# A hand-ordered four-layer kernel: the end of an LSTM reordered, and one event list across a batch norm

## The chip, the cores and the metric

One core of one Trainium2 chip. The metric is the device time of one launch in microseconds; lower is better. Engines in the text: PE (TensorE, the matrix array), DVE (VectorE), ACT (ScalarE), POOL (GpSimd), SP (SyncE, which issues most DMAs).

## What is computed

A residual tower of four layers over x, 128 batches of 64 nodes with 256 features, in float32. Each layer is `x = x + GNN(relu(layernorm(x)))`. The change lies at the end of layer 0 and in layer 1:

```python
# layer 0, its last part: LSTMs over windows of p nodes, p = 1..4
for p in range(1, MAX_SKIP + 1):
    nw = Tv // p
    wins = h[:, :nw * p, :].reshape(Bv * nw, p, Hd)
    last = _lstm_last(Wih[p - 1], Whh[p - 1], bih[p - 1], bhh[p - 1], wins)
    h = h.at[:, jnp.arange(nw) * p + (p - 1), :].set(last.reshape(Bv, nw, Hd))
#   one step:  i, f, g, o = split(x_t @ Wih.T + h @ Whh.T + bias)
#   c = sigmoid(f) * c + sigmoid(i) * tanh(g);   h = sigmoid(o) * tanh(c)

# layer 1, A_hat = the adjacency, normalized by degrees
agg = einsum("nm,bmd->bnd", A_hat, features)
h = relu(batchnorm(agg @ W1.T + b1))      # 256 -> 512, statistics over all 8192 rows
out = batchnorm(h @ W2.T + b2)            # 512 -> 256
```

Layers 2 and 3 (a graph convolution and causal attention) follow and are not touched. A batch norm needs the statistics of all rows before any row can go on: nothing of W2 can start on a channel until that channel is complete.

## The kernel before

**Tiles.** The 8192 rows are 16 super-tiles of 512 rows. Activations of layers 0 and 1 lie with channels on the partitions, in chunks of 128; each chunk of a super-tile is a 128x512 tile. The 256-wide hidden state has two chunks, the 512-wide middle of layer 1 four (numbered 0 to 3), handled in two halves (g = 0: chunks 0 and 1; g = 1: chunks 2 and 3). Matrix products of two super-tiles with a 256x256 block of weights are done in a scheme of seven products where eight would be plain. It needs sums of the weights (weight_sum, line 301 ff.: four POOL operations per weight) and of the data (T1 to T4: ag_sums at line 801 ff., and `sums` in second_product). The products carry numbers 1 to 7 and gather in three PSUM banks called a, b and c; DVE and ACT move the banks out in between (evict, add).

**Order.** There is no automatic scheduler. Events are put in a list by `at(t, fn)` with a time chosen by hand, sorted, and issued in that order; each engine then works through its own queue in order, and waits for data or for a free buffer. A time in the list decides only the order within each queue.

**LSTM.** `step` (line 717 ff.) does one time step for one state, a pair of blocks of 512 columns: the gates i, g, f, o one after another (`gate`: products on PE at L665 and L671, adds on DVE at L687, sigmoid and tanh on ACT at L683), then the cell: for each half n of the state, a multiply `keep` and an add `plus` (both at L710), tanh of the cell (L715), and `state` (L635), which writes h into the array hT that layer 1 reads. The operations of L710 run on POOL. Where `turn` is set (the last step of p = 2 and p = 3), DVE takes half n = 1. For p = 4 `turn` is always False. The last step of p = 4 on the second pair of groups ends the LSTM.

**The beginning of layer 1** is in the same list, behind `t -= 28` (line 792): `begin(s, t_load, t_turn, t_stats, t_relu, t_agg)` handles the first super-tiles of the class First: load x, transpose on PE (L541), add to x on DVE (L547), store, statistics on DVE (L564, L565), `root` (two operations on DVE at L569 and L570, two on POOL at L571 and L572), relu on ACT, aggregate on PE (L585). Super-tile 3 is turned at 30.6 and its statistics are taken at 36.1, between ag_sums of pair 0 (35.3, four sums on DVE, L810) and the last h (L635).

**Layer 1.** Products with W1 are in `half(i, g)` for pair i = 0 to 7: products L905, evictions by ACT L910, adds L913 and statistics L916 on DVE, in a rhythm GATE of 8.7 us per half; the last of the seven products of each half lies in the next half's time. PSUM is split in a pool of 5 banks ("gates") for these and one of 3 ("rest") for transposes and aggregates. After the last pair, `bn_coeffs` (L857 to L863) computes scale and shift for two chunks at a time: two bn_aggr, an add, three further small operations on DVE, and a power of -0.5 on POOL (L860). Then that list is issued, PSUM is made into one pool of 8 banks, weights of the later layers are loaded, and a second list holds the products with W2: `second_product(i)` has relu on ACT (L991; four operations on DVE at L987 and L989 in pair 0), the sums T1, T2, T3, T4 (L999 to L1005, for k = 0 on DVE, for k = 1 on POOL, except pair 0, all on DVE), products L1015 (k = 0 and k = 1: first and second half of the 512 channels), evictions L1019, adds L1022, statistics L1028. bn_coeffs of the second batch norm and layer 2 follow (L1078, L1112, L1121, L1173). The weight sums of W2 (L303) are issued on POOL just ahead of layer 1's list.

Of the kernel before, what the change touches and what calls it, by code (L numbers as in the profile page):

```python
# [14 lines left out]
P = 128  # L15
# [5 lines left out]
def kernel(ctx: ExitStack, tc: tile.TileContext, a: dict, out: bass.AP):  # L21
# [83 lines left out]
    mhalf = const.tile([P, 8], F32, tag="mhalf", name="mhalf")  # L105
    nc.gpsimd.memset(mhalf, -0.5)

    def block_diag(name, src):
# [490 lines left out]
    def at(t, fn, *args):  # L599
        events.append((t, len(events), fn, args))  # L600
# [116 lines left out]
    def step(t0, st, j, last, l, w, short_next):  # L717
# [20 lines left out]
        else:  # L738
# [4 lines left out]
            e, when, h_at = end["f"], (0, 6 * u, 11 * u), t + 8.6  # L743
            if short_next:
                keep_ = both(nc.vector.tensor_mul, st, "c", g["f"], "c")
                plus_ = both(nc.vector.tensor_add, st, "c", "c", g["g"])
                when, h_at = (0.4, 11.0, 12.0), t + 14.3
            for n in range(2):
                at(end["g"] + 0.1 * n, mul, n)
                at(e + when[0] * n, (keep, keep_)[n], n)  # L750
                at(e + when[0] * n + 0.1, (plus, plus_)[n], n)
# [20 lines left out]
    for p in range(1, NL + 1):  # L772
        l = p - 1
        if p < NL:
            at(t + 7.5, load, l + 1, 0)
            at(t + (40 if p == 1 else 64), lambda l=l: weight_sums(wt[l + 1][0][0]))
        if p > 1:
            at(t + 7.5, load, l, 1)
        whh_due = p > 1
        pairs = pairs_of(p)  # L780
        for k in range(0, len(pairs), 2):
            sts = [{"blk": blk, "N": blk[0][2] * GB, "p": p, "pool": pool}
                   for blk, pool in zip(pairs[k : k + 2], (lh0, lh1))]
            for j in range(p):
                for st in sts:
                    if j and whh_due:
                        whh_due = False
                        at(t - 6, lambda l=l: weight_sums(wt[l][1][0]))
                    turn = j == p - 1 and 1 < p < NL and k + 2 >= len(pairs)
                    t = step(t, st, j, j == p - 1, l, wt[l], turn)  # L790
# [21 lines left out]
    def begin(s, t_load, t_turn=None, t_stats=None, t_relu=None, t_agg=None):  # L812
# [8 lines left out]
        def stats():  # L821
            for q in range(Q):
                f.stats(q)
            f.root()

# [16 lines left out]
    begin(2, 13, 22.9, 23.0, 27.2)  # L842
    begin(3, 17, 30.6, 36.1)
    begin(4, 23)
    for k in range(4):
        at(t + 35.3 + 0.1 * k, ag_sums, 0, k, nc.vector)
# [5 lines left out]
    def bn_coeffs(pool, co, stats, c0, c1, prm, name):  # L852
# [10 lines left out]
        nc.vector.tensor_sub(shift, prm[:, 2, c0:c1], shift)  # L863

    co1 = const.tile([P, 3, HC], F32, tag="co1", name="co1")
    co2 = const.tile([P, 3, KC], F32, tag="co2", name="co2")
# [4 lines left out]
    with tc.tile_pool(name="pz", bufs=1, reuse_waits="tile") as pz:  # L871
# [8 lines left out]
        st2 = pz.tile([P, KC, NS, 6], F32, tag="st2", name="st2")  # L880
        for k in range(4):
            weight_sum(w2, k)

        new_banks(gates=5, rest=3)
        GATE = 8.7
        events = []

# [3 lines left out]
        def half(i, g):  # L893
# [23 lines left out]

            for t, name, j in ((0, "c", 2), (1.72, "a", 1), (3.46, "b", 5), (4.32, "a", 6),
                               (6.07, "b", 3), (6.93, "a", 7), (GATE + 0.86, "a", 4)):
                at(t0 + t, product, name, j)  # L920
            for t, fn, n, o, name in ((2.75, evict, 0, 0, "a"), (3.5, add, 0, 0, "c"),
                                      (4.5, evict, 1, 1, "b"), (5.35, evict, 1, 0, "a"),
                                      (7.1, add, 1, 0, "b"), (7.95, add, 1, 1, "a"),
                                      (GATE + 1.9, evict, 0, 1, "a")):
                at(t0 + t, fn, n, o, name)
            for t, n, o in ((5.5, 0, 0), (9.0, 1, 0), (9.7, 1, 1), (GATE + 2.9, 0, 1)):
                at(t0 + t, stats, n, o)
            if i == NS // 2 - 1:
                at(t0 + GATE + 3, bn_coeffs, lns, co1, st1, 2 * g, 2 * g + 2, con["bn1"], "bn1")

        for i in range(NS // 2):
            for g in range(2):
                half(i, g)
            for k, t in enumerate((-4.3, 0.9, 2.2, 3.5) if i else ()):
                at(GATE * 2 * i + t, ag_sums, i, k, nc.vector if i == NS // 2 - 1 else nc.gpsimd)
        for s in range(2, NS):
            f, t0 = First(s, "rest"), GATE * s
# [19 lines left out]

        for _, _, fn, args in sorted(events, key=lambda e: e[:2]):
            fn(*args)
        new_banks(psum=8)  # L960
        front.close()
        last.close()
        late = ctx.enter_context(tc.tile_pool(name="late", bufs=1, side="right", reuse_waits="tile"))
        adj4 = load_const("adj4", parts_d, [P, 4, P], late)
        adj3, smask = adj4[:, 0:3, :], adj4[:, 3, :]
        wl2 = [weight(f"wl2_{k}", a["W"][k], late) for k in range(3)]
        bl2 = row_bcast("bl2", a["bias"], D, late)
        wqk = late.tile([P, KC, D], F32, tag="wqk", name="wqk")
        aqk = late.tile([P, 7, P], F32, tag="aqk", name="aqk")
        wvo = late.tile([P, KC, D], F32, tag="wvo", name="wvo")  # L970
        wqkv = weight("wqkv", a["Wqkv"], late)
        wo = weight("wo", a["Wo"], late)

        events = []

        def second_product(i, tp):


            t0 = 7.0 * i
            tt, banks = {}, {}  # L980
# [3 lines left out]

            def relu(n, c):
                if i == 0 and n == 1 and c % 2 == 0:
                    nc.vector.tensor_scalar(z(n, c), z(n, c), co1[:, 0, c : c + 1],  # L987
                                            co1[:, 1, c : c + 1], op0=ALU.mult, op1=ALU.add)
                    nc.vector.tensor_scalar_max(z(n, c), z(n, c), 0.0)  # L989
                else:  # L990
                    nc.scalar.activation(z(n, c), z(n, c), AF.Relu, bias=co1[:, 1, c : c + 1],  # L991
                                         scale=co1[:, 0, c : c + 1])

            def sums(name, k, engine):
                if name != "T3" and name not in tt:
                    tt[name] = tp.tile([P, 2, SUP], F32, tag=name, name=name)
                b11, b21, b12, b22 = (z(n, 2 * k + c) for n in range(2) for c in range(2))
                if name == "T1":
                    engine.tensor_sub(tt["T1"][:, k], b12, b11)  # L999
                elif name == "T2":  # L1000
                    engine.tensor_sub(tt["T2"][:, k], b22, tt["T1"][:, k])
                elif name == "T3":
                    engine.tensor_sub(b12, b22, b12)
                else:
                    engine.tensor_sub(tt["T4"][:, k], b21, tt["T2"][:, k])  # L1005

            def product(name, j, ks=(0, 1)):
                new = name not in banks
                if new:
                    banks[name] = bank()  # L1010
                for k in ks:
                    x_ = (z(0, 2 * k), z(0, 2 * k + 1), z(1, 2 * k + 1),
                          *(tt[v][:, k] if v in tt else None for v in ("T4", "T1", "T2")),
                          z(1, 2 * k))[j - 1]
# [15 lines left out]
            def at(t, fn, *args):  # L1030
                events.append((t0 + t, len(events), fn, args))

            for k, (n, c) in enumerate(((0, 1), (0, 0), (0, 3), (0, 2), (1, 0), (1, 2), (1, 1), (1, 3))):
                at((-6.3, -5.8, -5.3, -4.4, -3.9, -3.4, -2.4, -1.9)[k], relu, n, c)
            for k, engine in enumerate((nc.vector, nc.gpsimd if i else nc.vector)):
                for name, t in (("T1", -2.8), ("T2", 0.1), ("T3", 0.6), ("T4", 1.6)):
                    at(t, sums, name, k, engine)
            for t, name, j in ((0, "c", 2), (1, "a", 1), (3, "b", 5), (5, "a", 6), (9, "a", 7),
                               (11, "b", 3), (13, "a", 4)):
                if i == 0 and t < 2:  # L1040
                    at(t, product, name, j, (0,))
                    at(t + 1.1, product, name, j, (1,))
                else:
                    at(t, product, name, j)
            at(2.2, lambda: evict(y(0, 0), 0, "a"))
            at(3.1, lambda: add(y(0, 0), y(0, 0), "c"))
            at(3.6, stats, 0, 0)
            at(4, lambda: evict(y(1, 1), 1, "b"))
            at(6, lambda: evict(tt["T2"][:, 0], 0, "a"))
            at(10, lambda: add(y(1, 1), y(1, 1), "a"))  # L1050
            at(10.5, stats, 1, 1)
            at(12, lambda: add(y(1, 0), tt["T2"][:, 0], "b"))
            at(12.5, stats, 1, 0)
            at(14.2, lambda: evict(y(0, 1), 1, "a"))
            at(15, stats, 0, 1)

        with tc.tile_pool(name="tp", bufs=2, reuse_waits="tile") as tp:
            for i in range(NS // 2):
                second_product(i, tp)
            for _, _, fn, args in sorted(events, key=lambda e: e[:2]):  # L1060
                fn(*args)
        bn_coeffs(lns, co2, st2, 0, KC, con["bn2"], "bn2")

# [355 lines left out]
```

## Time and profile before

| | |
|---|---|
| median of 3 runs | 1885.29 us (1885.29 to 1886.8) |
| profiled execution | 1886.4 us |
| its span, first to last instruction | 1884.5 us |
| mean granted TensorE clock | 0.997 |
| PE waits named in the trace, L905 (first batch norm's products) | 2.5 us and 1.9 us |
| PE waits on L1015 (products with W2) | 1.5 us and 0.9 us |
| bn_aggr (L857), 128x96 | 0.55 us each |
| pow on POOL (L860), 128x2 | 0.70 us |
| cell operation (L710) on POOL, 128x1024 | 2.35 us median |

In the trace all times are in microseconds from the start of the span. The LSTM's last products end at about 1218, layer 1's products with W1 run until 1359, those with W2 from 1361 to 1460. A row of the timeline gives start, length, engine, source line, operation, the tile written and the tiles read, the count, and in brackets the idle time before it and what ended it. Two PE instructions make one product of 128x128 by 128x512; in its steady rhythm such a product takes 0.86 us. The granted clock is a share of full speed.

### The profile page before, as it was taken

What the parts mean: (1) busy time and instruction counts of PE and PEld (TensorE: products, weight loads), DVE (VectorE), ACT (ScalarE), POOL (GpSimd) and SP (SyncE); (2) the same over time, 40 slices, a digit from 0 to 9 for tenths busy, and PEclk for the clock granted to TensorE, in tenths of its full rate; (3) what the DMA queues carried; (4) which work ended last, traced back from release to release, by engine and by line L of the source; (5) the groups of instructions that cost most, each with busy time, mean ns of one, the idle gap of its engine ahead of it and who ended that gap; (6) DMA issues with size and microseconds to landing.
All of it is one profiled execution on the core that took longest, in us unless ns stands there. A gap on an engine that the chain in (4) does not pass through costs nothing.

```text
span 1884.5 us, 19823 instructions
## 1 busy us (share of the span) xinstructions
PE 1859.9 (99%) x7080; PEld 1171.8 (62%) x7080; DVE 1137.3 (60%) x2268; ACT 923.2 (49%) x1591; POOL 643.0 (34%) x527
## 2 busy tenths in 40 slices
PE   8999999999999999999999999999999999999999
PEld 7997444444445666666444444556444788888887
DVE  6775777635546445435633333588787776677774
ACT  6775767534435434434533333478574344433442
POOL 4441422543324442422432222377253312211220
PEclk9999999999999999999999999999999999999999
DMA  5110001000001000000000000333200111111101
GB/s 145 57 57 0 1 1 38 8 1 0 1 0 45 1 0 1 1 1 22 1 0 1 1 0 22 101 112 112 70 1 1 46 45 45 35 46 45 46 23 34
DMA packets 50641, 54.85 MB, mean 29 GB/s; under 512 B 3184, under 2 KB 45936, under 8 KB 50544
## 3 DMA queue, kind: packets, MB, share of 16 engines
q1 hardware_dynamic: 50080, 53.40, 9.0%
q8 instruction: 56, 0.92, 0.2%
q14 instruction: 41, 0.34, 0.1%
q10 hardware_dynamic: 464, 0.20, 0.1%
HBM read 36.55 MB, written 17.04 MB: 28 GB/s over the span
## 4 chain that ended last, share of the span: by engine, by line
PE 94%; DVE 3%; ACT 1%; POOL 1%; DMA 1%; issue 0%; DVEq 0%; POOLq 0%
PE ps L665 34%; PE ps L671 19%; PE ps L1185 8%; PE ps L1015 5%; PE ps L905 5%; PE ps L1250 3%; PE ps L367 3%; PE ps L357 3%; PE ps L396 2%; PE ps L1226 2%; PE ps L1173 2%; PE ps L1260 2%; PE ps L585 1%; PE ps L1291 1%; PE ps L1198 1%; PE ps L541 1%
## 5 line engine op out<-in xcount | busy, mean ns | idle before, releaser
L687 DVE TENSOR_TENSOR gate<-gate,ps 128x512 f32<-128x512 f32 (+2 forms) x378 | 224.1, 620 | 446.9 <-PE ps L671 367.5
L665 PE MATMUL ps<-tx,wih 128*128 128x512 f32 (+2 forms) x1008 | 446.9, 542 | 2.7 <-ACT gate L690 1.0
L665 PE MATMUL ps<-hT,wih 128*128 128x512 f32 (+2 forms) x756 | 338.5, 541 | 0.0
L690 ACT COPY gate<-ps 128x512 f32<-128x512 f32 (+2 forms) x252 | 134.3, 533 | 378.7 <-PE ps L671 325.5
L665 PEld LDWEIGHTS ps<-tx,wih 128*128 128x128 f32 x1008 | 190.5, 190 | 193.3 <-issue 130.1
L683 ACT ACTIVATE gate<-gate,lbias 128x512 f32<-128x512 f32 (+2 forms) x252 | 216.7, 860 | 160.2 <-DVE gate L687 160.2
L671 PE MATMUL ps<-h,whh 128*128 128x512 f32 (+2 forms) x576 | 256.6, 527 | 0.0
L665 PEld LDWEIGHTS ps<-hT,wih 128*128 128x128 f32 x756 | 143.6, 190 | 141.6 <-issue 79.4
L671 PE MATMUL ps<-th,whh 128*128 128x512 f32 (+2 forms) x432 | 192.4, 527 | 0.0
L710 POOL TENSOR_TENSOR gate<-gate 128x1024 f32<-128x1024 f32 (+2 forms) x36 | 71.9, 2019 | 297.7 <-ACT gate L683 297.7
L1185 PE MATMUL ps<-wl,ag 128*128 128x256 f32 x768 | 172.1, 380 | 0.0
L671 PEld LDWEIGHTS ps<-h,whh 128*128 128x128 f32 x576 | 109.4, 190 | 100.2 <-issue 76.5
L1185 PEld LDWEIGHTS ps<-wl,ag 128*128 128x128 f32 x768 | 143.4, 190 | 20.2 <-ACT ag L1178 1.8
L710 POOL TENSOR_TENSOR cell<-gate 128x1024 f32<-128x1024 f32 (+2 forms) x36 | 79.4, 2227 | 175.2 <-ACT gate L683 175.2
L1141 POOL TENSOR_TENSOR ln_rn<-ln_rn,mhalf 128x4 f32<-128x4 f32 (+1 forms) x33 | 32.8, 993 | 300.7 <-DVE ln_rn L1140 300.1
L671 PEld LDWEIGHTS ps<-th,whh 128*128 128x128 f32 x432 | 82.1, 190 | 75.2 <-issue 57.4
L1148 ACT ACTIVATE h<-x,ln_rn 128x256 f32<-128x256 f32 x128 | 68.2, 594 | 101.1 <-DVE ln_rn L1144 101.1
L710 POOL TENSOR_TENSOR cell<-gate,cell 128x1024 f32<-128x1024 f32 (+2 forms) x32 | 65.1, 2052 | 110.2 <-ACT gate L683 110.2
L690 DVE COPY gate<-ps 128x512 f32<-128x512 f32 (+2 forms) x126 | 78.6, 624 | 20.8 <-PE ps L671 20.8
L715 ACT ACTIVATE gate<-cell 128x1024 f32<-128x1024 f32 (+2 forms) x72 | 68.1, 951 | 27.0 <-POOL cell L710 27.0
L683 ACT ACTIVATE gate<-ps,lbias 128x512 f32<-128x512 f32 (+2 forms) x126 | 79.5, 631 | 3.9 <-PE ps L671 1.0
L627 DVE TENSOR_TENSOR tx<-hT,tx 128x512 f32<-128x512 f32 (+2 forms) x72 | 59.1, 820 | 14.9 <-PE ps L665 10.2
(227 smaller groups left out, 2934.8 us busy)
## 6 DMA issues: line engine op xcount, KB each, us to landing
xt<-in_x_dram SPq DMA_DIRECT2D x30, 512.0 KB, 4.1
x1d<-xt SPq DMA_DIRECT2D x16, 512.0 KB, 3.0
x<-x1d SPq DMA_DIRECT2D x16, 512.0 KB, 4.8
out_dram<-x SPq DMA_DIRECT2D x15, 512.0 KB, 3.0
wih<-in_WihT_dram SPq DMA_DIRECT2D x16, 256.0 KB, 5.3
whh<-in_WhhT_dram SPq DMA_DIRECT2D x12, 256.0 KB, 5.4
xt<-in_x_dram SPq DMA_DIRECT2D x8, 128.0 KB, 3.6
wl<-in_W_dram SPq DMA_DIRECT2D x3, 256.0 KB, 3.9
```

The costliest lines, as they stand in the source:

```text
L627: yield nc.vector.tensor_sub(t[k], *((b[1][0], b[0][0]), (b[1][1], t[0]), (b[1][1], b[1][0]), (b[0][1], t[1 % len(t)]))[k])
L665: nc.tensor.matmul(wide(p_[:, :N]), wih[0][:, OF[k], gi, :], x_, start=first_, stop=(j == 0), skip_group_check=True)
L671: nc.tensor.matmul(p_[:, :N], whh[0][:, OF[k], gi, :], h_, start=False, stop=True, skip_group_check=True)
L683: nc.scalar.activation(to, r[bank_][:, :N] if bank_ else to, fn, bias=lbias[:, l, m : m + 1])
L687: nc.vector.tensor_add(slot(n, hc), slot(n, hc), r[bank_][:, :N])
L690: op(slot(n, hc), r[bank_][:, :N])
L710: fn(*((t["G"] if isinstance(t, dict) and "G" in t else st["c"])[:, n, :, : st["N"]] for t in tiles))
L715: nc.scalar.activation(o_, c, AF.Tanh)
L905: nc.tensor.matmul(r[name], con["w1"][:, OF[j], g, :], x_, start=new, stop=(name, j) in (("a", 4), ("b", 3), ("c", 2)), skip_group_check=True)
L1015: nc.tensor.matmul(banks[name], w2[:, OF[j], k, :], x_, start=(new and k == 0), stop=(k == 1), skip_group_check=True)
L1148: nc.scalar.activation(v[tag][:, q, :], v[src][:, q, :], AF.Relu, bias=v["rn"][:, 1, q : q + 1], scale=v["rn"][:, 0, q : q + 1])
L1185: nc.tensor.matmul(v["W"][:, q, :], v["ag"][:, c, m, ts(2 * k + q, P)], wl2[m][:, c, :], start=(n == 0), stop=(n == 3 * KC - 1))
```

## The change

1. In the last LSTM step's second state, `turn` is None: DVE takes the multiply and the add of half n = 1, and both tanh are placed after the sigmoids of gate o. The time of h stays.
2. Super-tile 3's transposes, adds, store and statistics are placed at 26.6 and 26.7 instead of 30.6 and 36.1. Its root stays at 36, after ag_sums.
3. The weight sums of W2 go from ahead of layer 1's list into it, two by two.
4. The first batch norm's coefficients are computed chunk by chunk, with bn_aggr on DVE and the other five operations on POOL.
5. The first products of W2 are in one list with the last ones of W1. The last pair of W1 has a tighter order of its own. The first halves (k = 0) of three products of pair 0 and of three of pair 1 come ahead of the second halves. The first T1 of both pairs go to a tile `early` in a buffer of xt. Banks are taken from "rest" for even pairs and from "gates" for odd ones. T3 is computed ahead of T2, and T2 from T3's result. One relu of pair 0 is on DVE, the others on ACT.

```diff
@@ top of the kernel @@
+    eps = const.tile([P, 1], F32, tag="eps", name="eps")
+    nc.gpsimd.memset(eps, EPS)
@@ step(), LSTM cell @@
-            if short_next:
+            if short_next is not False:
                 keep_ = both(nc.vector.tensor_mul, st, "c", g["f"], "c")
                 plus_ = both(nc.vector.tensor_add, st, "c", "c", g["g"])
                 when, h_at = (0.4, 11.0, 12.0), t + 14.3
+            if short_next is None:
+                when, h_at = (4.2, 6.6, 7.4), t + 8.6
@@ the loop over p, states and steps @@
-                    turn = j == p - 1 and 1 < p < NL and k + 2 >= len(pairs)
+                    turn = j == p - 1 and p > 1 and k + 2 >= len(pairs)
+                    if p == NL and turn:
+                        turn = None if st is sts[-1] else False
@@ begin() and the calls of it @@
             for q in range(Q):
                 f.stats(q)
-            f.root()
+            if s != 3:
+                f.root()
...
-    begin(3, 17, 30.6, 36.1)
+    begin(3, 17, 26.6, 26.7)
     begin(4, 23)
+    at(t + 36, lambda: First(3).root())
@@ coefficients of the first batch norm, one chunk at a time @@
+    def bn_coeffs1(c):
+        mv = lns.tile([P, 2], F32, tag=f"bn1mv{c}", name="bn1mv", bufs=1)
+        nc.vector.bn_aggr(mv, st1[:, c, :, :].rearrange("p s k -> p (s k)"))
+        scale, shift, v = (co1[:, k, c : c + 1] for k in range(3))
+        nc.gpsimd.tensor_add(v, mv[:, 1:2], eps)
+        nc.gpsimd.tensor_tensor(v, v, mhalf[:, :1], ALU.pow)
+        nc.gpsimd.tensor_mul(scale, v, con["bn1"][:, 1, c : c + 1])
+        nc.gpsimd.tensor_mul(shift, mv[:, 0:1], scale)
+        nc.gpsimd.tensor_sub(shift, con["bn1"][:, 2, c : c + 1], shift)
@@ layer 1 @@
-        for k in range(4):
-            weight_sum(w2, k)
...
+            end = i == NS // 2 - 1
+            if end:
+                t0 = B + 6.02 * g
+            late_a = 6.1 if g else 6.9
+            for t, name, j in (((0, "c", 2), (1.72, "a", 1), (2.58, "b", 5), (3.44, "a", 6), (4.3, "b", 3),
+                                (5.16, "a", 7), (late_a, "a", 4)) if end else
...
-            if i == NS // 2 - 1:
-                at(t0 + GATE + 3, bn_coeffs, lns, co1, st1, 2 * g, 2 * g + 2, con["bn1"], "bn1")
+            if end:
+                at(t0 + (7.9 if g else 7.35), bn_coeffs1, 2 * g)
+                at(t0 + 9.2, bn_coeffs1, 2 * g + 1)
...
+        for k in range(4):
+            at(GATE * (4 + 2 * (k // 2)) + 9.7 + 0.8 * (k % 2), weight_sum, w2, k)
...
-        new_banks(psum=8)
@@ second_product, now in the list of the first @@
+            t0 = B + 10.32 + slot * (7.0 * i - 1.5 if i > 1 else (-1, 5.5)[i])
...
+                elif name == "T3":
+                    engine.tensor_sub(b12, b22, b12)
+                elif name == "T2":
+                    engine.tensor_add(sum_of("T2", k), b12, b11)
...
+                    banks[name] = bank("gates" if i % 2 else "rest")
...
+            if i < 2:
+                for t, name, j in (((12.9, "a", 1), (13.76, "b", 5), (14.6, "c", 2)) if i == 0 else
+                                   ((15.5, "a", 1), (16.3, "c", 2), (17.2, "b", 5))):
+                    at_us(t, product, name, j, (0,))
...
+                if i == 0:
+                    at_us(17.4, relu, 1, 1, True)
+                for t, name, k in (((12.6, "T1", 0), (18.4, "T3", 0), (19.0, "T2", 0), (19.6, "T1", 1),
+                                    (20.2, "T3", 1), (20.5, "T2", 1), (21.4, "T4", 0), (22.0, "T4", 1))
+                                   if i == 0 else
+                                   ((16.7, "T1", 0), (24.9, "T3", 0), (25.5, "T2", 0), (26.1, "T4", 0))):
+                    at_us(t, sums, name, k, nc.vector)
...
+                for t, name, j in (((18.06, "a", 1), (18.92, "c", 2), (19.78, "b", 5)) if i == 0 else
+                                   ((22.4, "c", 2), (23.2, "a", 1), (25.8, "b", 5))):
+                    at_us(t, product, name, j, (1,))
...
+        emit(B + 18.0)
         front.close()
         last.close()
...
+        with tc.tile_pool(name="tp", bufs=2, reuse_waits="tile") as tp_:
+            tp.append(tp_)
+            emit(1e9)
+        new_banks(psum=8)
         bn_coeffs(lns, co2, st2, 0, KC, con["bn2"], "bn2")
```

## The prediction

> **What bounds the kernel now.** First the page's head and busy shares, then the waits, since one engine fills nearly the whole span:
>
> ```profile
> span 1884.5 us, 19823 instructions
> PE 1859.9 (99%) x7080; PEld 1171.8 (62%) x7080; DVE 1137.3 (60%) x2268; ACT 923.2 (49%) x1591; POOL 643.0 (34%) x527
> ```
>
> TensorE is busy 1859.9 of 1884.5 us, so only 24.6 us of idle exist anywhere, plus whatever it loses at a lower clock while it counts as busy. The change adds and removes no matmul. It can gain only where PE waits or runs slow, and the waits of PE say where that is:
>
> ```profile
> PE ps L357 <- ACT ln_h L349: 6.9, 1, 6.9
> PE ps L905 <- DVE hS L913: 2.5, 1, 2.5
> PE ps L905 <- DVE z L913: 1.9, 1, 1.9
> PE ps L1121 <- DVE hS L1112: 1.8, 1, 1.8
> PE ps L1015 <- ACT hS L991: 1.5, 1, 1.5
> PE ps L1015 <- ACT hS L1019: 0.9, 1, 0.9
> ```
>
> (waited in all, times, longest). The first is the kernel's start and the fourth is the second batch norm; the change touches neither. The second is the end of the LSTM; the third, fifth and sixth are the batch norm in the middle of layer 1. Together 6.8 us. PE's timeline at both places (start, length, count of PE instructions, two per matmul of 512 columns; the bracket is idle before):
>
> ```profile
> 1226.91 1.02 PE L905 MATMUL ps<-ag,w 128*128 128x512 f32 x2
> 1230.42 1.30 PE L905 MATMUL ps<-T,w 128*128 128x512 f32 x2 [2.48 <-DVE hS L913]
> 1231.51 1.92 PE L905 MATMUL ps<-ag,w 128*128 128x512 f32 x2
> 1233.22 1.74 PE L585 MATMUL ps<-ahT,h 128*128 128x128 f32 x8
> 1234.80 1.02 PE L905 MATMUL ps<-T,w 128*128 128x512 f32 x2
> ...
> 1357.99 1.12 PE L905 MATMUL ps<-T,w 128*128 128x512 f32 x2 [1.85 <-DVE z L913]
> 1360.59 3.47 PE L1015 MATMUL ps<-hS,w 128*128 128x512 f32 x4 [1.48 <-ACT hS L991]
> 1363.97 2.16 PE L1015 MATMUL ps<-z,w 128*128 128x512 f32 x4
> ```
>
> After each wait the same instructions take about twice as long: the eight L585 1.74 us where the row at 1226.02 has 1.05. Table by stretch, granted clock third from the end:
>
> ```profile
> 1230.00:1235.00 5.00, 4.58 (x13) 2.93 (x14) 4.06 (x10) 1.38 (x3) 3.05 (x3) 0.66 0.23 84
> 1361.00:1365.00 4.00, 4.00 (x6) 1.33 (x5) 3.02 (x11) 2.14 (x4) 0.70 (x1) 0.58 0.10 35
> ```
>
> 0.66 and 0.58, where the 110 us between have 1.00: a pause costs its length and then a slow stretch.
>
> **Part 1, end of the LSTM.** The bank that the matmul at 1230.42 needs is freed by DVE's third L913. DVE's rows ahead of it: gate add ends 1217.31; idle 1.18; first sum L810 2.55 us (the other three 0.69 each), because POOL runs cell operations (L710) until 1220.48; eight statistics of super-tile 3, 1222.89 to 1225.1 (2.2); root; four L635 from 1225.36, and five adds and statistics.
>
> ```profile
> 1218.49 2.55 DVE L810 TENSOR_TENSOR T<-ag 128x512 f32<-128x512 f32 x1 [1.18 <-PE ps L671]
> 1215.81 4.67 POOL L710 TENSOR_TENSOR cell<-cell,gate 128x1024 f32<-128x1024 f32 x2
> ```
>
> - Shared cell: POOL keeps one multiply and one add (1211.17 to 1215.85) and DVE takes the other two, 1.22 us each (the multiply at 530.00, from an earlier shared step), 2.5 with the gap. They start when the gate adds end and fill the 1.18 idle. POOL has stopped by then, so L810 drops from 2.55 to 0.69 (1.86).
> - Super-tile 3 earlier: its eight transposes (0.90 us of PE) only change places with products. The two adds L547 (1.27) and the statistics (2.2) go before the last gate adds, into an idle stretch of DVE. Its store moves with them on SP's queue, in unchanged order; its x (DMA to xt) has landed by about 1193. The gate adds come about 0.15 earlier.
> - ACT runs both tanh after the last sigmoids: the second follows the cell's end at 1219.7 and closes near 1221.8, ahead of L635.
>
> L635 then starts earlier by 1.18 + 1.86 + 2.2 + 0.15 + 0.1 (small gaps) - 2.5 = 3.0: 1222.36 for 1225.36. The five microseconds from there to the bank's release stay, so PE goes on at 1227.42 for 1230.42 and waits about 0.4 for 2.48.
>
> Next the slow stretch. From 1230.42 to 1234.80 PE does four L905 (0.43 each) and eight L585 (0.89): 2.61 of work in 4.38, 1.77 lost. [...] The row shows the slow clock after both, so I take 3.0 + 1.77 = **4.8** and expect a wait of 0.4 not to bring it back. Ends: 3.0 (slow stretch stays) and 5.2 (wait goes entirely).
>
> [...] DVE's add at 531.33 took 3.18, not 1.22. By that price the 3.0 would shrink to 1.0. Here I don't apply it: POOL starts 1211.17 and ends 1215.85, DVE's multiply starts at 1217.2. 1.3 us of margin.
>
> **Part 2, w2's weight sums.** Four POOL operations (L303, 3.34 us at 1227.27) move into layer 1's steady part, in pairs of 1.67, into POOL gaps of 4.04 us (1266.72 to 1270.76, for one). Cost zero; without that gap, ag_sums would be late by up to 1.7 twice. At the old place, POOL's next row (L553) starts up to 3.3 earlier, which no one waits for. The eps tile costs one small write at the start: zero.
>
> **Part 3, one list over the batch norm.** From 1357.99 to 1370.60 PE does the last product (0.86) and the first eight matmuls of W2 (16 instructions, 6.88): 7.74 of work in 12.61, after a wait of 1.85.
>
> - DVE now does four bn_aggr (0.55 each) and no more; add, pow, two multiplies and a subtract are POOL's, on 128x1. Before, DVE spent 1352.84 to 1355.42 on the first pair of chunks with 0.81 waiting for pow, and the adds L913 stood behind it. Of these 2.58 two bn_aggr stay (1.10); the adds then wait for their own products only, and in the walk of the written order the third L913 ends 1.06 earlier: PE's last product starts at 1356.93.
> - POOL's price per chunk: pow takes 1.01 on four columns and 0.70 on two, so I estimate 0.54 on one; the other four 0.20 each (the 128x4 multiply L572); gaps 0.07: 1.6 us. The walk gives chunks ready at 1353.1, 1355.1, 1360.95 and 1362.6. POOL was idle there for 20.3 and 6.95 us, so nothing is queued behind them; ACT's relus wait for them.
> - The first two pairs of super-tiles begin with their first-half products, which need chunks 0 and 1 alone. Three of pair 0 and three of pair 1 fill PE while chunks 2 and 3 are made. Their relus (0.71 each on ACT) are done in time, and one goes to DVE. Banks come from pools of 3 and 5 instead of 8; in the walk each is freed well ahead.
> - PE then runs from 1356.93 without a long pause: 7.74 of work and waits of 0.28 (first product that needs chunk 3) and 0.12 (sums on POOL): the eighth matmul is done at 1365.07 for 1370.60. **5.5**.
> - Uncertain: POOL's small operations read SBUF beside DVE's sums[...]. Chunk 3 has 0.3 of slack. Taking 0.5 off I use **5.0**. Ends: 6.0 (no waits) and 3.5 (about 0.7 for each of the last chunks and some wait at the join).
> - T2 is now made from T3's result: same count and length. In the steady rows POOL's T2 sum at 1392.26 is followed by its product only near 1403; 1.3 later still leaves some 9 us. The steady part, 12.03 us per pair on PE alone, stays. So does the second batch norm with its 1.77 wait and slow stretch (1467 to 1470, clock 0.50).
>
> **Sum.** 4.8 + 0 + 5.0 = 9.8. Profiled execution: 1886.4 (span 1884.5 and 1.9 around it) becomes 1876.6. The median of the runs is 1885.29, 1.1 below that execution: **1875.5**.
>
> **Rivals.**
> 1. *The slow clock stays or moves (0.25).* For it: [...] the second batch norm's slow stretch could also grow. Against: rows with 0.94 idle (1368.78) show no slow stretch after. Then only the idles count: 3.0 and, of part 3, 1.06 + 1.48 + 0.94 - 0.4 = 3.1: 6.1, 1879.2.
> 2. *A new wait replaces the old (0.14).* POOL's chain, in series over chunks, is delayed[...], or early banks are freed late, and PE waits 1.5 to 2 at chunk 2 or 3 and slows once more: part 3 gives 1.5 to 2 and the whole 6.5, 1878.8. For it: 0.3 of slack. Against: POOL idle on both sides.
> 3. *Slower (0.03).* The second product's steady part now takes each pair's banks from a pool of 3 or of 5. If a 3-bank pair had to wait for ACT's or DVE's eviction, PE would pause in pairs 2, 4 and 6, and follow-on waits in the rest. From 1.6 us per pair over six pairs it eats the 9.8; at 2.5 the kernel takes 1875.5 + 15 = 1890.5. Against: the waits in the walked order end some 6 us before PE arrives, and a pair needs three banks at a time.
> 4. *Nothing won at the LSTM end (0.03).* L635 was bound by tanh, not by DVE: then 5.0 alone, 1880.3. Against: tanh ended 1221.81 in the trace, 3.5 before L635.
>
> **Numbers.** Likeliest, as summed: 0.55, 1873.5 to 1877.5. Lower end of range: 5.2 + 6.0 and up to 1.7 if the last slow stretch (3.4 us of work at half speed) should not occur, 1872.4, rounded to 1872. Upper: rivals 1, 2 and 4 with their bounds, 1880.5. Beyond 0.2% (3.8 us, about what this measurement can tell from no change): faster 0.93, same 0.04, slower 0.03.
>
> **What would show it.** PE's waits on L913 (hS) at 0.5 or less, clock 1.00 after it; L810 at 0.69 for the first sum; DVE's two cell rows at 1.2; L1112's wait unchanged at 1.8. In part 3 the waits on L991 and L1019 gone, PE's L1015 in its 0.86 rhythm and no clock under 0.9 between 1350 and 1460. Wrong if: DVE's cell add takes over 2 us, POOL's five operations take over 2.5 a chunk, or 12.03 per pair grows.

## The result, and the profile after

The kernel after takes 1878.27 us (1878.18 to 1878.46), beside 1886.05 (1885.29 to 1887.32) for the kernel before in the same measurement: a ratio of 0.9958 (95% interval 0.9941 to 0.9975), 7.8 us less where 9.8 was forecast. That lies in the stated range of 1872 to 1880.5, above its likeliest part (1873.5 to 1877.5). Its profiled execution took 1878.31 with a span of 1876.6, 7.9 less than the span of before.

PE's waits in the profile after (waited in all, times, longest):

```profile
PE ps L359 <- DMA xt<-in_x_dram: 7.4, 1, 7.4
PE ps L1197 <- DVE hS L1188: 1.8, 1, 1.8
...
PE ps L1039 <- ACT z L1007: 0.9, 1, 0.9
...
PE ps L922 <- DVE z L930: 0.8, 1, 0.8
...
PE ps L1039 <- POOL T L1027: 0.4, 1, 0.4
PE ps L922 <- DVE hS L930: 0.3, 1, 0.3
PE ps L1039 <- DVE T L1023: 0.3, 1, 0.3
```

The 2.5 of the LSTM's end is now 0.3, the 1.9 is 0.8, and the 1.5 and 0.9 at W2's products (L1039, before L1015) have become 0.9, 0.4 and 0.3. PE's timeline at both places:

```profile
1226.30 1.03 PE L922 MATMUL ps<-ag,w 128*128 128x512 f32 x2
1227.67 1.12 PE L922 MATMUL ps<-T,w 128*128 128x512 f32 x2 [0.34 <-DVE hS L930]
1228.63 1.02 PE L922 MATMUL ps<-ag,w 128*128 128x512 f32 x2
1229.49 1.05 PE L587 MATMUL ps<-ahT,h 128*128 128x128 f32 x8
1230.38 1.88 PE L922 MATMUL ps<-T,w 128*128 128x512 f32 x4
...
1352.50 1.12 PE L922 MATMUL ps<-T,w 128*128 128x512 f32 x2 [0.78 <-DVE z L930]
...
1360.50 1.13 PE L1039 MATMUL ps<-z,w 128*128 128x512 f32 x2 [0.87 <-ACT z L1007]
1361.93 2.84 PE L1039 MATMUL ps<-T,w 128*128 128x512 f32 x6 [0.30 <-DVE T L1023]
...
1372.17 2.84 PE L1039 MATMUL ps<-T,w 128*128 128x512 f32 x6 [0.38 <-POOL T L1027]
```

The eight L587 are back at 1.05, and no stretch between 1225 and 1450 has a clock under 1.00.

Three marks on PE cut every trace into four stretches that can be compared: A from the start to the last LSTM step's first product on hT (L665; L667 in after), B from there to the T products behind the eight aggregates at about 1230, C from there to the second batch norm's first transposes (L1121; L1197), D to the end of the span. B holds the LSTM's end, C all of layer 1; of what the change touches, A holds the eps tile and the moved work of super-tile 3 (its transposes go from 1213.73 to 1206.97, the same work for PE), and D nothing.

| trace | A | B | C | D | median, us |
|---|---|---|---|---|---|
| before | 1214.63 | 20.17 | 230.73 | 418.97 | 1886.05 |
| after | 1214.88 | 15.50 | 227.39 | 418.83 | 1878.27 |
| b2_before_again | 1216.86 | 18.50 | 230.73 | 418.81 | 1886.85 (one run) |
| a2_after_again | 1215.39 | 15.50 | 227.41 | 418.90 | 1878.94 |
| e1_lstm_end | 1215.19 | 15.49 | 231.16 | 418.86 | 1882.47 |
| e2_bn_list | 1215.17 | 20.18 | 227.39 | 418.86 | 1883.10 |
| e3_cell_only | 1215.51 | 17.75 | 227.39 | 418.95 | 1881.37 |
| e4_st3_only | 1215.33 | 16.14 | 227.40 | 418.63 | 1879.26 |
| e5_act_order | 1215.13 | 15.50 | 226.62 | 418.95 | 1877.63 |
| e7_relu_act | 1215.27 | 15.49 | 226.57 | 418.87 | 1878.10 |
| e6_both | 1215.45 | 15.50 | 225.97 | 418.88 | 1877.34 |
| e8_pair1 | 1215.59 | 15.51 | 225.70 | 419.00 | 1877.02 |
| e9_w2_old | 1215.14 | 15.50 | 227.40 | 418.86 | 1878.77 |
| e10_pairwise | 1215.65 | 15.50 | 227.73 | 419.32 | 1879.96 |

B and C repeat within 0.02 wherever the code and the clock are the same. A doesn't: it differs by up to 2.2 us between two executions of one kernel. So effects of some tenths are read from B and C, and the medians of runs, which carry A, only back them up.

### The profile page after: what moved, and what is told of

Read it like the earlier page. It is cut to its first block, busy times and chain, and to the rows that moved or that the text cites. A ratio compares the mean times of both kernels' runs of the same rounds, so it can differ in the third digit from the quotient of the medians.

```text
span 1876.6 us, 19835 instructions
## 1 busy us (share of the span) xinstructions
PE 1856.1 (99%) x7080; PEld 1171.4 (62%) x7080; DVE 1129.8 (60%) x2260; ACT 923.8 (49%) x1592; POOL 642.5 (34%) x544
## 4 chain that ended last, share of the span: by engine, by line
PE 93%; DVE 3%; POOL 1%; ACT 1%; issue 1%; DMA 1%; SPq 0%; DVEq 0%; POOLq 0%; ACTq 0%
PE ps L667 34%; PE ps L673 19%; PE ps L1261 8%; PE ps L922 4%; PE ps L1039 4%; PE ps L369 3%; PE ps L359 3%; PE ps L1326 3%; PE ps L398 2%; PE ps L1249 2%; PE ps L1302 2%; PE ps L1336 2%; PE ps L1367 1%; PE ps L587 1%; PE ps L1274 1%; PE ps L1197 1%
## 5 line engine op out<-in xcount | busy, mean ns | idle before, releaser
L667 PE MATMUL ps<-tx,wih 128*128 128x512 f32 (+2 forms) x1008 | 447.0, 542 | 2.7 <-ACT gate L692 1.0
L667 PE MATMUL ps<-hT,wih 128*128 128x512 f32 (+2 forms) x756 | 338.7, 541 | 0.0
L667 PEld LDWEIGHTS ps<-tx,wih 128*128 128x128 f32 x1008 | 190.7, 190 | 192.4 <-issue 129.5
L667 PEld LDWEIGHTS ps<-hT,wih 128*128 128x128 f32 x756 | 143.7, 190 | 141.4 <-issue 79.3
```

Source lines behind the costliest of these rows:

```text
L667: nc.tensor.matmul(wide(p_[:, :N]), wih[0][:, OF[k], gi, :], x_, start=first_, stop=(j == 0), skip_group_check=True)
```

## The experiments

**The two parts alone.** e1_lstm_end is the kernel before with parts 1 and 2 of the list of changes (shared cell, super-tile 3 early):

```diff
-            if short_next:
+            if short_next is not False:
...
-    begin(3, 17, 30.6, 36.1)
+    begin(3, 17, 26.6, 26.7)
...
+    at(t + 36, lambda: First(3).root())
```

> The kernel before with only the LSTM end changed (shared cell and super-tile 3 early). My theory: the two parts of the change add up, and this one gives the shift seen in the trace after, 4.42 us (4.66 if its later start by 0.24 is left out of it), so 4.4 to 4.8 below before; PE's wait at the first T products falls to 0.3 to 0.5, no slow clock follows, and the first batch norm keeps its waits of 1.9, 1.5 and 0.9 and its slow stretch. Rival[...]: the batch norm's slow stretch changes with the shift, and the sum lies between 3 and 6.5 below before.

1882.47 (1881.86 to 1883.37) beside 1886.45 (1884.81 to 1888.35): 4.0 less; ratio 0.9981 (0.9973 to 0.9988). B falls by 4.68. C grows by 0.43: the batch norm's slow stretch is twice as long here (from 1354.43 to 1361.26) and begins within the pauses (clock 0.68 from 1353 to 1357 and 0.50 in the four us after). So the total fell short of the 4.4 to 4.8 expected: the clock's slow stretch changed with the shift, as the rival had it.

e2_bn_list is the kernel after with these edits taken back.

> The kernel after with the LSTM end of before, so only the list across the batch norm and the moved weight sums. My theory: 3.3 us below before (1.07 from earlier coefficients of the first chunks, 3.18 up to the eighth matmul of W2, 0.9 given back in the two pairs after it); the LSTM end keeps its wait of 2.5 and its stretch at a clock of 0.66; POOL's operations for chunk 3 are as long as in the trace after, since they meet the same DVE operations. Rival (POOL was only delayed by phase): the chain for chunk 3 takes 1.65 and the part gives about 4.8.

1883.10 (1881.34 to 1884.17), 3.35 below before; ratio 0.9981 (0.9973 to 0.9988). B is 20.18 again with its wait of 2.48 and a clock of 0.68, C is 227.39 to the hundredth, and the chain for chunk 3 is as long as in after. 4.0 and 3.35 make 7.35, and the whole change gives 7.8 (1878.27) or 7.4 (1878.94 beside 1886.35 in the last measurement): the parts add up within what the medians can tell.

**Inside the LSTM's end.** e3_cell_only takes back the early super-tile 3 alone:

```diff
-            if s != 3:
-                f.root()
+            f.root()
...
-    begin(3, 17, 26.6, 26.7)
+    begin(3, 17, 30.6, 36.1)
...
-    at(t + 36, lambda: First(3).root())
```

> The kernel after with super-tile 3 back at its late place; the cell stays shared. My theory (what counts is DVE's queue ahead of the h writes): the 2.2 us of statistics stand ahead of the writes again, PE waits about 2.4 to 2.6, and the slow clock comes back with some 1.8: 3.8 to 4.2 slower than after. Rival[...]: only the idle time comes back, 2.2 slower than after.

1881.37 (1880.43 to 1883.48). The wait is 2.48 again, and the clock stays at 1.00 behind it. PE's timeline of e3_cell_only:

```profile
1230.55 1.13 PE L920 MATMUL ps<-T,w 128*128 128x512 f32 x2 [2.48 <-DVE hS L928]
1231.51 1.02 PE L920 MATMUL ps<-ag,w 128*128 128x512 f32 x2
1232.37 1.05 PE L587 MATMUL ps<-ahT,h 128*128 128x128 f32 x8
```

B is 2.25 longer than in after: in this trace only the idle time came back, as the rival had it. The median is 3.1 above after, between the two numbers, as it would be if some executions had the slow stretch; one trace can't show that.

e4_st3_only leaves the cell on POOL and keeps super-tile 3 early:

```diff
-            if short_next is not False:
+            if short_next:
...
-            if short_next is None:
-                when, h_at = (4.2, 6.6, 7.4), t + 8.6
...
-                    turn = j == p - 1 and p > 1 and k + 2 >= len(pairs)
-                    if p == NL and turn:
-                        turn = None if st is sts[-1] else False
+                    turn = j == p - 1 and 1 < p < NL and k + 2 >= len(pairs)
```

> The kernel after with all four cell operations on POOL; super-tile 3 stays early. My theory: DVE's first sum is 2.5 us long again behind POOL's last add, and the h writes start about 0.85 later: PE waits about 1.2, and it is 0.9 slower than after if that wait brings no slow stretch, 2.6 if it does. Rival (sharing the cell is what gains, as the shared tanh comes earlier): over 3 slower than after, with the writes waiting for ACT.

1879.26 (1879.19 to 1879.37), 1.0 above after; B is 0.64 longer. DVE's rows in e4_st3_only, then in after:

```profile
1218.96 2.75 DVE L812 TENSOR_TENSOR T<-ag 128x512 f32<-128x512 f32 x1 [0.96 <-PE ps L673]
```

```profile
1217.47 1.22 DVE L712 TENSOR_TENSOR cell<-gate,cell 128x1024 f32<-128x1024 f32 x1
1218.79 1.23 DVE L712 TENSOR_TENSOR cell<-cell,gate 128x1024 f32<-128x1024 f32 x1
1219.94 0.68 DVE L816 TENSOR_TENSOR T<-ag 128x512 f32<-128x512 f32 x1
```

With the cell on POOL, DVE first stands idle for 0.96, and then the first sum takes 2.75 beside POOL's cell add: 3.70 from the end of the last gate add to the end of the sum. Shared, DVE does two cell operations and the sum in 3.06. Sharing is worth 0.64 of the 3.0 (0.75 with super-tile 3 late: B is 18.50 in b2_before_again, below, and 17.75 in e3); the early super-tile, 2.25 to 2.36, is the larger part. The expected wait of 1.2 did not show as one. PE is held in three places: 0.24 for DVE's sum and 0.23 for ACT's eviction ahead of the old place, and there 1.16 go by from start to start for 0.86 of work.

**The clock.** The kernel before was profiled again.

> The kernel before once more, for a second profile. My theory (the slow stretch after the 2.48 pause depends on where the pause falls, as the cell-only kernel had the pause and a clock of 1.00): pauses of 2.48 and 1.85 as in the first profile, and at least one of the three slow stretches (after 1230, 1361 and 1467) is missing or has another clock; the time then differs by 1.5 to 2 us per stretch. Rival (a slow stretch always follows a pause of this length): clocks of 0.66, 0.58 and 0.50 as before, and the same time within 0.5.

1886.85. The same pause of 2.47, and this time no slow stretch behind it; the one in the batch norm is there. PE's timeline and a stretch of the batch norm (granted clock third from the end) in b2_before_again:

```profile
1232.64 1.13 PE L905 MATMUL ps<-T,w 128*128 128x512 f32 x2 [2.47 <-DVE hS L913]
1233.61 1.02 PE L905 MATMUL ps<-ag,w 128*128 128x512 f32 x2
1234.46 1.05 PE L585 MATMUL ps<-ahT,h 128*128 128x128 f32 x8
```

```profile
1361.00:1365.00 4.00, 3.73 (x5) 1.39 (x6) 3.05 (x10) 2.14 (x4) 0.70 (x1) 0.59 0.25 81
```

B is 18.50, 1.67 less than in the first trace. So the same pause is followed by a slow stretch in two traces (before, e2) and not in two (b2, e3).

What decides it can be read from the traces, which record every change of the granted clock. In all 14 of them these changes lie on a fixed grid of 3.413 us. In before, for one, the slow stretches last 3.413 each, and the stretches at full speed between them 126.29, 102.40 and 413.01: 37, 30 and 121 times as much. Only the grid's place against the program differs from one execution to the next: an edge lies at 1231.23 in before and at 1232.00 in b2. Two neighbouring windows of this grid at the pause, in before and then in b2_before_again (length, busy time of PE first, granted clock third from the end):

```profile
1227.82:1231.23 3.41, 0.93 (x3) 0.49 (x3) 3.38 (x7) 2.08 (x5) 3.33 (x5) 1.00 0.00 0
1231.23:1234.65 3.42, 3.42 (x10) 2.10 (x9) 2.48 (x7) 1.37 (x2) 1.82 (x2) 0.50 0.23 86
```

```profile
1228.59:1232.00 3.41, 1.58 (x9) 0.75 (x7) 3.38 (x7) 2.43 (x5) 3.25 (x5) 1.00 0.00 0
1232.00:1235.42 3.42, 2.78 (x13) 1.82 (x14) 3.02 (x8) 1.51 (x3) 3.31 (x4) 1.00 0.00 0
```

In before, as in e2, the whole pause lies in one window, and the next window runs at half speed. In b2 an edge cuts it into 1.83 and 0.65, in e3 into 1.68 and 0.80, and no slow window follows. The same count over all windows of the clock's record in the 14 traces (it begins at 12.7 us in before, at 12.3 in after): each of the 22 at full speed in which PE was idle for 1.88 us or more is followed by a slow one, and none of those with 1.70 or less; of the nine in between, three are. In before, the windows from 1357.53 and 1463.34, with 1.94 and 1.90 idle, are followed by a slow one and the window from 1354.11, with 1.40, is not; in after the one from 1456.12, with 1.78, is. I estimate the border from these counts at 1.85, to about a tenth, since the ends of matmuls are modelled: in these traces a little over half of a window of 3.413 sufficed. In after, the waits of 0.87 and 0.30 may fall into one window, as they do in e9_w2_old; that makes 1.18, and no slow window follows.

The total of b2 is no lower because its first 25 us took 2.2 longer, with waits of 0.90, 0.51 and 0.39 that the first trace has not.

The kernel after was run again as well.

> The kernel after once more, for a second profile and more times. My theory (what differs between executions lies in the first 25 us and in slow stretches after long pauses; after has no long pause left in what was changed): from the LSTM's last step to the last product of W2 every start is as in the first profile, relative to it, within 0.1, with a clock of 1.00; the median is 1877.8 to 1878.8 and the lowest and highest time are less than 2 apart, where before's are 3 to 3.5 apart. Rival (the slow stretches come back at random after short waits too): a clock under 0.9 somewhere between 1225 and 1450, and a spread as wide as before's.

1878.94 (1878.76 to 1879.19) beside 1886.35. B and C as in the first trace, clock 1.00 from 1225 to 1450, A 0.5 longer. The two sets of times together spread over 1.0, those of before over 3.4 in one measurement. No trace with a wait of 0.33 or 0.34 at the LSTM's end (nine of them) has a slow stretch there, as the border would have it.

**Where the batch norm's part lost 1.7.** POOL's rows for the last two chunks in after, with DVE's beside the last one:

```profile
1354.80 0.19 POOL L878 TENSOR_TENSOR co<-bn1mv,eps 128x1 f32<-128x1 f32 x1 [3.96 <-DVE bn1mv L876]
1355.07 0.55 POOL L879 TENSOR_TENSOR co<-co,mhalf 128x1 f32<-128x1 f32 x1
1355.70 0.19 POOL L880 TENSOR_TENSOR co<-co,bn 128x1 f32<-128x1 f32 x1
...
1356.38 0.19 POOL L878 TENSOR_TENSOR co<-bn1mv,eps 128x1 f32<-128x1 f32 x1
1356.64 1.03 POOL L879 TENSOR_TENSOR co<-co,mhalf 128x1 f32<-128x1 f32 x1
1357.75 0.39 POOL L880 TENSOR_TENSOR co<-co,bn 128x1 f32<-128x1 f32 x1
1358.22 0.65 POOL L881 TENSOR_TENSOR co<-bn1mv,co 128x1 f32<-128x1 f32 x1
1358.95 0.65 POOL L882 TENSOR_TENSOR co<-bn,co 128x1 f32<-128x1 f32 x1
```

```profile
1356.49 0.69 DVE L1023 TENSOR_TENSOR early<-hS 128x512 f32<-128x512 f32 x1 [0.59 <-ACT hS L1007]
1357.10 0.54 DVE L1003 TENSOR_SCALAR hS<-hS,co 128x512 f32<-128x512 f32 x1
1357.67 0.43 DVE L1005 TENSOR_SCALAR hS<-hS 128x512 f32<-128x512 f32 x1
1358.13 0.69 DVE L1025 TENSOR_TENSOR hS<-hS 128x512 f32<-128x512 f32 x1
1358.86 0.69 DVE L1027 TENSOR_TENSOR T<-hS 128x512 f32<-128x512 f32 x1
```

For chunk 2, with only DVE's statistics and bn_aggr beside it (1354.64 to 1355.90), the chain takes 1.63 (1354.80 to 1356.43); for chunk 3 it takes 3.22, and three of POOL's operations end within 0.05 of the end of a DVE operation: L880 with L1005, L881 with L1025, L882 with L1027. ACT's relu of chunk 3 starts at 1359.63, and PE waits for it. Three kernels try this.

e7_relu_act moves the relu of L1003 and L1005 to ACT:

```diff
-                    at_us(17.4, relu, 1, 1, True)
+                    at_us(17.2, relu, 1, 1)
```

> The kernel after with relu (1,1) of pair 0 on ACT instead of DVE, all else as it is. My theory (what holds POOL up is mainly DVE's sums[...]): these start somewhat earlier and meet POOL's last two operations as before; chunk 3 is ready 0.2 earlier, 0.2 below after. Rival (DVE's relu[...] is what holds POOL up): chunk 3 is ready 1 us earlier, 0.8 or more below after.

1878.10 (1877.07 to 1878.64); C is 0.82 shorter, the rival's number; the median, 0.17 below after's, hides it, since A is 0.39 longer. The chain took 2.38 (1356.77 to 1359.15), its last three rows in e7_relu_act:

```profile
1358.05 0.19 POOL L880 TENSOR_TENSOR co<-co,bn 128x1 f32<-128x1 f32 x1
1358.32 0.19 POOL L881 TENSOR_TENSOR co<-bn1mv,co 128x1 f32<-128x1 f32 x1
1358.59 0.56 POOL L882 TENSOR_TENSOR co<-bn,co 128x1 f32<-128x1 f32 x1
```

Of the 0.84, pow gave 0.10 and L880 0.20, which DVE's relu had held. L881 gave 0.46, because with this lead it starts 0.08 ahead of the sum L1025 (1358.40) and no longer behind it; L882 still meets that sum. My theory named the sums as the cause. In these rows they held POOL's operation only where they came first (L881 0.65 in after, L882 0.65 in after and 0.56 in e7, for 0.19), so that the 0.3 which POOL gained on pow and L880 became 0.8. The rival is right on the size.

e5_act_order changes ACT's order alone:

```diff
-                for t, n, c in (((11.0, 0, 0), (11.8, 1, 0), (13.0, 0, 1), (17.0, 0, 2), (17.6, 0, 3),
-                                 (18.5, 1, 2), (19.3, 1, 3)) if i == 0 else
+                for t, n, c in (((11.0, 0, 0), (11.8, 1, 0), (13.0, 0, 1), (17.0, 0, 2), (17.1, 1, 2),
+                                 (17.6, 0, 3), (19.3, 1, 3)) if i == 0 else
```

> The kernel after with one change: in pair 0, ACT makes relu (1,2), which needs chunk 2 alone, ahead of relu (0,3), in the 2.4 us in which it stands waiting for chunk 3's coefficients. My theory (the wait of 0.30, 0.57 with the restart, at the first product of T1's second half hangs on ACT's order): that wait goes, 0.5 to 0.6 below after; the wait of 0.87 stays. Rival (that wait is DVE's queue, held up by sums beside POOL): no change.

1877.63 (1876.93 to 1878.33); C is 0.77 shorter, a little more than the 0.5 to 0.6 expected. The wait of 0.30 is gone, that of 0.87 stays (0.88), and the one of 0.38 falls to 0.32.

e6_both has both edits, and T1's second half between T3 and T2.

> The kernel after with relu (1,2) ahead of (0,3), and relu (1,1) on ACT instead of DVE, so that DVE's sums T3 and T2 come only after POOL has finished chunk 3; T1's second half is placed between T3 and T2. My theory (POOL's five operations for chunk 3 take 3.2 us instead of 1.65[...], and this is PE's wait of 0.87): the chain for chunk 3 ends about 1.1 earlier, the waits of 0.87 and 0.30 both go, 1.2 to 1.6 below after. Rival (ACT becomes the bound with one more relu): the waits stay at 0.5 or more and the gain is under 0.6.

1877.34 (1877.17 to 1877.79); C is 1.42 shorter, the waits of 0.87 and 0.30 are gone. L880 to L882 take 0.19 each, pow 0.94 where chunk 2's takes 0.55: the sum `early`, from 1357.06 to 1357.75, still meets it (from 1357.23). ACT, with one more relu, did not become the bound.

e8_pair1 adds one thing for the wait of 0.38 in pair 1:

```diff
-                                 (23.5, 1, 2), (24.3, 1, 1), (25.1, 1, 3))):
+                                 (23.5, 1, 2), (24.3, 1, 1), (24.8, 1, 3))):
```

> The kernel of the run e6_both with one more change: in pair 1, ACT makes relu (1,3) ahead of pair 2's first relu (0,1), so that POOL's sums T3 and T2 for pair 1 start 0.7 earlier. My theory (PE's wait of 0.40, 0.55 with the restart, hangs on that relu's place in ACT's queue): the wait goes, 0.4 to 0.6 below e6_both, about 9.6 below before. Rival (POOL's sums stand behind DVE's sums[...] anyway): the wait stays above 0.2 and the time within 0.2 of e6_both.

1877.02 (1876.88 to 1877.48) beside 1886.93: ratio 0.995 (0.9936 to 0.9963), the lowest of all. C is 0.27 shorter than in e6_both, less than expected: the wait on POOL's T2 is gone, and 0.16 on ACT's eviction L1043 is next.

**Two parts expected to matter little.** e9_w2_old puts the weight sums of W2 back ahead of layer 1's list.

> The kernel after with the four weight sums of W2 back ahead of layer 1's list. My theory (POOL has a gap either way): the shift from the LSTM's end to the last products of W1 stays within 0.1 of after, and the time within 0.4. Rival (at the old place they delay the next sums on POOL and with them PE, now that PE comes 4.7 earlier): a wait of PE on layer 1's first pairs and 0.5 to 2 slower than after.

1878.77 (1878.26 to 1879.21), B 15.50 and C 227.40: no effect, as forecast.

e10_pairwise has the old coefficients, two chunks at a time, in the new list:

```diff
-                at(t0 + (7.9 if g else 7.35), bn_coeffs1, 2 * g)
-                at(t0 + 9.2, bn_coeffs1, 2 * g + 1)
+                at(t0 + 9.2, bn_coeffs, lns, co1, st1, 2 * g, 2 * g + 2, con["bn1"], "bn1")
```

> The kernel after with the coefficients of the first batch norm computed as before, two chunks at a time, small operations on DVE and the power on POOL, in the new list. My theory (what gains is that first halves of W2's products fill the time of the last chunks; POOL's chain for chunk 3, 3.2 long, costs as much as DVE's stop for the pair): PE's wait before the last product of W1 grows by 0.7 to 1.0, that of 0.87 goes, one of about 0.5 comes at T1 of pair 1; within 0.6 of after. Rival (the chunk-wise coefficients are what gains): 1.5 or more slower than after.

PE's timeline in e10_pairwise:

```profile
1354.33 1.12 PE L922 MATMUL ps<-T,w 128*128 128x512 f32 x2 [1.85 <-DVE z L930]
...
1360.06 1.13 PE L1038 MATMUL ps<-early,w 128*128 128x512 f32 x2 [0.31 <-DVE early L1022]
1361.02 1.88 PE L1038 MATMUL ps<-z,w 128*128 128x512 f32 x4
```

The wait before the last product is 1.85 again, 1.07 more, one of 0.31 comes at `early`, and the 0.87 is gone: C is 0.34 longer than in after. The median, 1879.96 (1879.56 to 1880.98), is 1.7 above after and 1.0 above its second set. Its A is 0.77 longer than after's and its D 0.49; the first is ahead of all that differs, and most of the second lies in the last store of the output (from its issue at 1873.89 to the end 4.35, in after 3.90). By C, computing the coefficients by chunk is worth 0.34 of the 3.34 in this list; with the old coefficients the new order alone gives 3.00.

## Why the prediction was right or wrong

- **What bounds it.** Right: B and C hold the whole gain, 4.67 and 3.34 in the traces; A and D, which hold the first and the fourth wait, don't change by more than they do between executions.
- **LSTM end, 3.0 of order.** Right to the hundredth where the clock is 1.00 on both sides: 18.50 - 15.50. The DVE operations came at 1.22 and 1.23, the sum at 0.68, L635 2.75 earlier in the trace and 3.0 with A's 0.25 taken off, the wait at 0.34 for 0.4. DVE's and POOL's cell operations did not overlap (POOL ended at 1216.21, DVE began at 1217.47), so the longer times that the prediction feared had no occasion.
- **The slow stretch, 1.77.** Its size was right (1.67 between the two traces of before), but it was counted as certain: two pauses of 2.5 in four have it, depending on their place on the clock's grid. With a border of 1.85, a pause of 2.48 placed at random on a grid of 3.41 brings it in 0.64 of cases. This is an estimate from the traces' numbers (3.413, 2.48 and the estimated border): for 0.93 of the 3.41 the whole pause lies in one window, and for 0.63 on either side enough of it does. The term would then be 1.1. The sum was also made wrongly from there: the median of 1885.29 that I subtracted from need not be an execution with that stretch. The change does take the slow stretch away. That the first trace of before had it, so that B gave 4.67 for 4.8, was partly luck.
- **Weight sums, eps tile.** Right: zero (e9).
- **First chunks and the last product of W1.** 1.06 forecast, 1.07 measured (1357.99 - 1352.50 is 5.49, of which B and A gave 4.42).
- **W2's first products.** This is the term that was mis-sized, 5.0 for 3.34 in C. The step: "chunks ready at 1353.1, 1355.1, 1360.95 and 1362.6", 1.6 each. The duration alone was right (1.63, pow 0.55 for 0.54), but chunk 3 met five DVE operations and took 3.22. I had named this and priced it at 0.5, with waits of 0.28 and 0.12; PE lost 1.03 at the wait and, with the relu order behind it, 0.57 at the next, so that the eighth matmul came 4.25 earlier (the 1.07 included) for 5.5. My own sign of being wrong, over 2.5 a chunk on POOL, came true for this chunk. The pairs behind gave back another 0.9, which the sum had put at nothing.
- **T2 from T3's result, "some 9 us" of slack.** Right in the steady pairs, wrong in pair 1, whose POOL chain starts only when ACT gets to its relus: a wait of 0.38, 0.55 with the restart (explained at the end), and the larger part of the 0.9. The steady pairs keep their 12.02.
- **Second batch norm.** Its wait stays at 1.78. Its slow stretch (clock 0.63 from 1460 to 1464 in after) was priced at 1.7 in the low end, wrongly: from the first transposes to L1249 after takes 5.66, and a2, with no slow stretch, 5.63, where PE waits 1.59 for ACT's relu instead. It was hidden.
- **Rivals.** The second (a new wait at chunk 3) came true in part: 0.87 at the place it named, without a slow clock. The first has it right that the slow stretch can move: in e1 the batch norm's begins at 1354.43, in before at 1360.94. In after it did not stay. The slower one didn't occur: the steady rhythm keeps its 0.86 per product, and no steady wait for banks appears.

## What to carry to other kernels

When an in-order engine takes over small operations, price them beside what the neighbour engine runs at that very moment, not alone: here a chain of five operations of 0.19 to 0.55 doubled. Before counting a slow-clock stretch as gain, see how much of the pause falls into one window of the clock (3.413 us here), and look for it in a second trace. Compare by stretches between marks in the trace, since start-up alone moved one kernel by 2 us. And where an engine waits for one input, let it do first what needs another: two such swaps on ACT (0.77 and 0.27) were worth more than the larger idea of coefficients by chunk (0.34).

## What the hardware showed unexpectedly

- POOL's small multiply L880 took 0.39 instead of 0.19 beside DVE's maximum L1005 (0.43 for 512 columns), and 0.19 once that was on ACT (e7). L1003 held pow by 0.10 at most: pow took 1.03 beside it in after and 0.93 in e7. I had reckoned only with DVE's sums.
- In after, a wait of PE cost more than its row: the one of 0.87 cost 1.03 from the end of the last matmul's work (1358.61 and two of 0.43) to the next start, since a row ends 0.16 later than its work; 0.57 for the 0.30, since the instruction behind the previous wait also took 0.11 longer.
- One kernel's first 25 us differed by 2.2 between two executions, and these times lie in no stretch that a change of this kind touches.
